# A transformer chain with experts on one core: runs of small passes placed more closely, the last layer's inverse roots on another engine, and one maximum read from PSUM

## The chip, the core and the metric

The kernel runs on one core of a Trainium2 chip. It has five engines that work side by side, each in the order of its own instruction stream: TensorE (PE: matmuls and transposes, results in PSUM), VectorE (DVE), ScalarE (ACT: activation functions, copies), GpSimd (POOL[...]) and SyncE (SP: DMA issue). The metric is the device time of one execution in microseconds (us). The time before is the median of three runs, 1779.1 us (1774.51 to 1781.71).

## The reference, cut to what matters

The input is `x`, 64 sequences of 64 tokens with 128 features, and a context `ctx` of the same shape. Four layers follow each other:

```python
# layer 0: self attention over [ctx, x] with 16 heads of 64 and relative positions, norm, relu feed-forward, norm
# layer 1: masked self attention, norm, masked cross attention with ctx, norm, relu feed-forward, norm (heads of 8)
# layer 2: gate between a token and its sequence's pooled context, softmax over the tokens, norm
# layer 3:
x = x + mha(ln(x), ln(x))                     # self, 16 heads of 8
x = x + mha(ln(x), ln(ctx))                   # cross, both sides normed
h = ln(x)
vals, idx = top_k(h @ rw.T + rb, 2)           # router: 2 of 8 experts
gates = softmax(vals)
x = x + sum over the 2 of gates * (gelu(h @ fc1[e].T + b1[e]) @ fc2[e].T + b2[e])

def ln(x): return (x - mean(x)) / sqrt(var(x) + 1e-5) * g + b
```

All arithmetic is float32.

## The kernel before

**Tiling.** The 4096 tokens are eight groups (`g` = 0 to 7) of 512: a tile `x0` to `x7` of 128 partitions by four blocks of 128 features. Layer 0 runs first with all engines held to program order. Everything after it is made of Python generators, driven by one function.

**The driver.** `drive` (L149) keeps two lists of tasks: "attention" (`self1`, `cross1`, `self3`, `cross3`, each for every group, all groups of one phase before the next phase) and "light" (`forward1`, `layer2`). A task is started every four or two turns of the loop, once the same group has finished its earlier phase. In each turn every running generator is advanced to its next `yield`, and the generator `experts` (called `fill`) is advanced once, or two and three times by turns after the last exponentials have been issued. So a `yield` sets how finely a task's instructions are mixed with those of others. The instructions so recorded then pass a planner that orders each engine's stream by the estimated readiness and the order of recording; the queues on the chip are in order.

**A norm.** `normalise` (L263) takes mean and variance of four blocks on VectorE, adds epsilon there, raises to the power -0.5 on GpSimd (`rs`, 128x4), multiplies the mean by it on VectorE (`nmr`) and scales on ScalarE (`z` or `zx`). It is used for all norms. In the last layer `ln_turned` (L1230) calls it for the self attention's input, and for the query and context of the cross attention; `cross3` (L1251) calls it once more for the router's input `zx`. That makes 32 calls of 80.

**Attention with small heads.** `small_heads` forms keys `km` and queries `qs` on ScalarE, scores in four PSUM banks (`sc`), and for each bank the maximum of each row (`mx`) and the difference. Without a mask (last layer), the first three banks are read by VectorE straight from PSUM; the fourth is copied by ScalarE to SBUF (`s`), VectorE takes the maximum from that copy and GpSimd subtracts. The weights are turned on TensorE (`pt`), ScalarE takes the exponential (`pT`), and `av` multiplies them with the values.

**Router and experts.** `router` (L1279) takes the logits (`pl`), the two largest, the gates, each token's row in a table of experts (`pr` counts by a triangular matmul), and scatters the rows to `hrows` in DRAM: eight indirect DMAs per group, issued by GpSimd. `experts` (L649) waits until groups 0 to 4 have been routed, makes a `table` of 47 blocks of 128 rows, waits until the last group's exponentials have been issued, and then handles one block in each step: a load from `hrows` (SyncE), a transpose (`xt`), `f<-fcw,vp` (first matmul), transposes (`ht`), Gelu on ScalarE, the second matmul, and a scatter to `yrows` by GpSimd out of one of six result buffers. A second table of 31 blocks follows when groups 5 to 7 have been routed. Finished rows are read back, summed with `x` and written out.

Nearly all instructions carry line L74 in the profile, since one helper issues them; the groups are told apart by the names of their tiles.

Of the kernel before, what the change touches and what calls it, by code (L numbers as in the profile page):

```python
# [12 lines left out]
AF = mybir.ActivationFunctionType  # L13
# [3 lines left out]
P = 128  # L17
# [77 lines left out]
def kernel(ctx: ExitStack, tc: tile.TileContext, a: dict, out: bass.AP):  # L95
# [13 lines left out]
    def ctile(shape, name, dtype=F32):  # L109
        return const.tile(shape, dtype, tag=name, name=name)  # L110
# [34 lines left out]
    def mid(ap, n):  # L145

        return ap.unsqueeze(1).to_broadcast([ap.shape[0], n, ap.shape[1]])

    def drive(phases, lags, ends, fill):  # L149

        todo = {kind: [] for kind in lags}
        for n, (start, kind) in enumerate(phases):
            for g in range(NG):
                todo[kind].append((n, g, start))

        todo["light"].sort(key=lambda task: task[1])
        passed = {(-1, g) for g in range(NG)} - {(-1, g) for g, gen in ends}
        count = 0
        running, wait = [(-1, g, gen) for g, gen in ends], {kind: 0 for kind in lags}
        while running or any(todo.values()):
            for kind, tasks in todo.items():
                if wait[kind] <= 0:
                    for task in tasks:
                        n, g, start = task
                        if (n - 1, g) in passed:  # L170
                            tasks.remove(task)
                            running.append((n, g, start(g)))
                            wait[kind] = lags[kind] - (kind == "attention" and not todo["light"])
                            break
                wait[kind] -= 1
            for task in list(running):
                n, g, gen = task
                if next(gen, "end") == "end":
                    running.remove(task)
                    passed.add((n, g))  # L180
            count += 1
            for _ in range(2 + count % 2 if done["exponentials"] else 1):
                next(fill, "end")
        for _ in fill:
            pass

# [15 lines left out]
    make_identity(nc, ident[:, :])  # L202
    nhalf = ctile([P, NBLK], "nhalf")
    nc.gpsimd.memset(nhalf, -0.5)
    xs = [ctile([P, T], f"x{g}") for g in range(NG)]
    bd_small = ctile([P, 6, 8], "bd_small")
    bd = ctile([P, 6, P], "bd")
# [52 lines left out]
        nc.scalar.copy(t, pt)  # L260
        return t

    def normalise(dst, src, npm=None, width=D):  # L263

        st = wtile([P, NBLK, 6], "st6", 4)
        mv = wtile([P, NBLK, 2], "mv", 4)
        rs = wtile([P, NBLK], "rs", 4)
        for k in range(NBLK):
            nc.vector.bn_stats(st[:, k, :], src[:, k * P : (k + 1) * P])
        for k in range(NBLK):  # L270
            nc.vector.bn_aggr(mv[:, k, :], st[:, k, :])
        nc.vector.tensor_scalar(
            rs, mv[:, :, 1:2].rearrange("p a b -> p (a b)"), EPS, None, ALU.add
        )
        nc.gpsimd.tensor_tensor(rs, rs, nhalf, ALU.pow)
        if npm is not None:
            nc.gpsimd.tensor_tensor(rs, rs, npm, ALU.mult)
        yield
        if npm is None:
            nm = wtile([P, NBLK], "nmr", 4)  # L280
            nc.vector.scalar_tensor_tensor(
                nm, mv[:, :, 0:1].rearrange("p a b -> p (a b)"), -1.0, rs, op0=ALU.mult, op1=ALU.mult
            )
        for k in range(NBLK):
            ks = slice(k * P, (k + 1) * P)
            if npm is None:
                nc.scalar.activation(
                    dst[:, k * width : k * width + D], src[:, ks], AF.Identity,
                    scale=rs[:, k : k + 1], bias=nm[:, k : k + 1],
                )  # L290
            else:
                nc.vector.tensor_scalar(
                    dst[:, ks], src[:, ks], mv[:, k, 0:1], rs[:, k : k + 1], ALU.subtract, ALU.mult
                )
# [354 lines left out]
    def experts():  # L649
# [160 lines left out]

        while done["routed"] < PARTS[0]:
            yield
        yield from table(0)
        while not done["exponentials"]:
            yield

# [5 lines left out]
        for t in range(-6, total + 3):  # L822
# [1 line left out]
            while h < NH and done["routed"] < sum(PARTS[: h + 1]):  # L824
                yield
            if h < NH and h not in tables:
                yield from table(h)
            if t + 6 < total:
                load(t + 6)
            if 0 <= t < total:  # L830
# [25 lines left out]
    def other_layers(ends):  # L856
# [65 lines left out]
        def small_heads(qT, kvT, wq, wk, wv, wo, scale, bias=None, maskb=None, then=None):  # L922
# [28 lines left out]
            def scores(hb):  # L951
# [13 lines left out]
                for g in (3, 0, 1, 2):  # L965
# [10 lines left out]
                    elif g == 3:  # L976
                        nc.scalar.copy(s, s3)
                    if maskb is not None or g == 3:
                        nc.vector.tensor_reduce(mx, s, axis=AX.X, op=ALU.max)
                        nc.gpsimd.tensor_tensor(s, s, last(mx[:, :], S), ALU.subtract)  # L980
                    else:
                        nc.vector.tensor_reduce(mx, s3, axis=AX.X, op=ALU.max)
# [247 lines left out]
        def ln_turned(src, g, b, z=None):  # L1230

            z = wtile([P, T], "z", 3) if z is None else z
            yield from normalise(z, src)
            yield
            pt = transpose4(z)
            t = wtile([P, T], "T", 4)
# [14 lines left out]
        def cross3(g):  # L1251
# [16 lines left out]
            yield  # L1268

            zx = wtile([P, NBLK, ROWW], "zx", 4)  # L1270
            yield from normalise(zx.rearrange("p k c -> p (k c)"), x, width=ROWW)
            yield
            pt = transpose4(zx.rearrange("p k c -> p (k c)"), ROWW)
            hT = wtile([P, T], "T", 4)
            nc.scalar.activation(hT, pt, AF.Identity, scale=col("moe_g"), bias=col("moe_b"))
            yield
            yield from router(g, hT, x, zx)

        def router(g, hT, x, zx):  # L1279

# [220 lines left out]
```

## Time and profile before

| what | value |
|---|---|
| median of three runs | 1779.1 us |
| the profiled execution's own time | 1766.36 us |
| its span in the profile | 1764.6 us |
| granted TensorE clock, mean | 0.943 |
| busy: TensorE, its weight loads | 1617.1 us (92%), 1166.4 us (66%) |
| busy: VectorE, ScalarE, GpSimd | 1214.6 (69%), 991.9 (56%), 913.1 us (52%) |
| `pow` of the norms on GpSimd | 80, 1020 ns each |
| table loads on ScalarE | 2, 1283 ns each |

The profile lists for each engine the busy time and for each group of like instructions: line, engine, operation, output and inputs by the program's names, shape, count, then the busy time and mean duration, and after the second bar the idle time of that engine just ahead of these instructions with what ended it. A busy TensorE is not TensorE at its peak: the ends of matmuls are modelled. PEclk is the clock granted to TensorE; the records show 1.0 or 0.5 at any time. A table load (ACT_TABLE_LOAD) brings a set of functions into ScalarE; it is put into the stream by the compiler where the next function is not in the set that is loaded.

### The profile page before, as it was taken

What the parts mean: (1) busy time and instruction counts of PE and PEld (TensorE: products, weight loads), DVE (VectorE), ACT (ScalarE), POOL (GpSimd) and SP (SyncE); (2) the same over time, 40 slices, a digit from 0 to 9 for tenths busy, and PEclk for the clock granted to TensorE, in tenths of its full rate; (3) what the DMA queues carried; (4) which work ended last, traced back from release to release, by engine and by line L of the source; (5) the groups of instructions that cost most, each with busy time, mean ns of one, the idle gap of its engine ahead of it and who ended that gap; (6) DMA issues with size and microseconds to landing.
All of it is one profiled execution on the core that took longest, in us unless ns stands there. A gap on an engine that the chain in (4) does not pass through costs nothing.

```text
span 1764.6 us, 46242 instructions
## 1 busy us (share of the span) xinstructions
PE 1617.1 (92%) x18026; PEld 1166.4 (66%) x18026; DVE 1214.6 (69%) x3289; ACT 991.9 (56%) x2712; POOL 913.1 (52%) x875
## 2 busy tenths in 40 slices
PE   7799999999999999699998999899888988679995
PEld 4466666666666666477776777667666767557774
DVE  4567686867676767578887786777566874556663
ACT  4365555556464646255665555567677853236663
POOL 2446373737374647467776666444222243554454
PEclk9899999999999999899999998899889987579998
DMA  6756555555545455410010000000000000112143
GB/s 160 159 142 158 127 142 132 136 138 131 139 128 141 132 147 153 138 49 8 11 32 25 23 20 8 13 2 2 8 14 14 2 20 20 55 51 56 54 122 89
DMA packets 215160, 136.78 MB, mean 78 GB/s; under 512 B 38896, under 2 KB 198786, under 8 KB 214816
## 3 DMA queue, kind: packets, MB, share of 16 engines
q1 hardware_dynamic: 186880, 90.54, 21.3%
q10 hardware_dynamic: 23520, 34.75, 6.0%
q0 software_dynamic: 4544, 8.54, 1.4%
q8 instruction: 144, 2.36, 0.6%
q14 instruction: 72, 0.59, 0.1%
HBM read 66.51 MB, written 68.19 MB: 76 GB/s over the span
## 4 chain that ended last, share of the span: by engine, by line
PE 64%; DVE 16%; ACT 7%; POOL 5%; issue 3%; DMA 3%; another core or an unknown queue 0%; SPq 0%; POOLq 0%; ACTq 0%; DVEq 0%
PE av L74 8%; PE psv L74 8%; PE proj L74 7%; PE psk L74 6%; PE pt L74 6%; PE f L74 6%; PE tok L74 5%; PE pbd L74 4%; DVE mx L74 3%; PE psc L74 3%; DVE s L74 3%; PE acc L74 3%; PE sc L74 3%; ACT z L74 3%; PE tr L74 2%
## 5 line engine op out<-in xcount | busy, mean ns | idle before, releaser
L74 ACT ACTIVATE s<-s,nm 128x128 f32<-128x128 f32 x512 | 198.0, 388 | 248.9 <-DVE nm L74 218.7
L74 POOL TENSOR_TENSOR s<-s,sm 128x512 f32<-128x512 f32 x128 | 130.4, 1040 | 256.0 <-DVE sm L74 256.0
L74 PE MATMUL pt<-ident,s 128*128 128x128 f32 x1536 | 213.5, 282 | 24.5 <-ACT kT L74 10.4
L74 POOL TENSOR_TENSOR s<-s,mx 128x512 f32<-128x512 f32 x160 | 164.0, 1045 | 107.1 <-DVE mx L74 106.9
L74 PEld LDWEIGHTS pt<-ident,s 128*128 128x128 f32 x1536 | 176.4, 145 | 45.1 <-issue 15.2
L74 ACT ACTIVATE pT<-pt 128x512 f32<-128x512 f32 x256 | 141.7, 605 | 81.6 <-PE pt L74 76.9
L74 POOL TENSOR_TENSOR rs<-rs,nhalf 128x4 f32<-128x4 f32 x80 | 81.6, 1020 | 191.9 <-DVE rs L74 157.8
L74 POOL TENSOR_TENSOR skew<-skew,mb 128x512 f32<-128x512 f32 x128 | 159.9, 1271 | 37.0 <-DMA skew<-scr 36.5
L74 PEld LDWEIGHTS av<-vb,pT 128*64 128x64 f32 x4096 | 133.7, 144 | 21.2 <-issue 16.5
L74 PE MATMUL av<-vb,pT 128*64 128x18 f32 x4096 | 142.0, 216 | 4.7 <-issue 2.6
L74 DVE TENSOR_REDUCE mx<-s 128x8 f32<-128x512 f32 x160 | 102.9, 675 | 43.8 <-ACT s L74 43.8
L74 POOL DMA_INDIRECT yrows<-km,tob x78 | 76.2, 977 | 100.9 <-DVE m L74 75.3
L74 PE MATMUL psv<-wv,kv 128*128 128x256 f32 x512 | 127.4, 392 | 0.0
L74 PE MATMUL psk<-kv,wk 128*128 128x512 f32 x256 | 127.4, 620 | 0.0
L74 PE MATMUL sc<-km,qs 32*64 32x256 f32 x2048 | 104.7, 420 | 17.2 <-ACT qs L74 12.6
L74 DVE COPY pT<-pt 128x512 f32<-128x512 f32 x128 | 82.2, 683 | 37.5 <-PE pt L74 37.5
L74 PEld LDWEIGHTS psv<-wv,kv 128*128 128x128 f32 x512 | 92.2, 189 | 15.1 <-issue 1.0
L74 PEld LDWEIGHTS av<-pT,v 128*64 128x64 f32 x2048 | 66.6, 138 | 52.8 <-issue 31.1
L74 PEld LDWEIGHTS pbd<-rT,qp 64*128 64x128 f32 x1024 | 63.0, 189 | 58.0 <-DVE qp L74 56.3
L74 DVE TENSOR_TENSOR s<-sc,mb 128x512 f32<-128x512 f32 x128 | 81.9, 680 | 23.1 <-PE sc L74 23.1
L74 DVE TENSOR_TENSOR s<-psc,skew 128x512 f32<-128x512 f32 x128 | 87.5, 683 | 14.7 <-issue 7.3
L74 ACT ACTIVATE z<-z,nmr,rs 128x128 f32<-128x128 f32 x160 | 66.1, 488 | 55.7 <-DVE nmr L74 42.0
(237 smaller groups left out, 3749.0 us busy)
## 6 DMA issues: line engine op xcount, KB each, us to landing
scr<-stage SPq DMA_DIRECT2D x64, 516.0 KB
skew<-scr SPq DMA_DIRECT2D x128, 256.0 KB
hrows<-pad ACTq DMA_DIRECT2D x66, 330.0 KB
ctx<-in_ctxT SPq DMA_DIRECT2D x24, 256.0 KB
km<-hrows SPq DMA_DIRECT2D x78, 66.0 KB
fcw<-in_fc ACTq DMA_DIRECT2D x16, 256.0 KB
kv<-in_xT SPq DMA_DIRECT2D x8, 256.0 KB
kv<-in_ctxT SPq DMA_DIRECT2D x8, 256.0 KB
```

Of the source, the lines that this page charges most:

```text
L74: ins = it(*args, **kw)
```

## The change

There are three parts.

1. The driver knows a new word, `CHAIN`. A task that yields it is in a run of small passes: it is not advanced with the others but behind every second other piece of a turn, at the end of the turn, and behind every step of `experts`. The norm and transposes ahead of the router, the router itself and both tables are such runs.
2. `normalise` has a second way to the inverse root, `root="ln"`: Ln of variance plus epsilon and Exp with a scale of -0.5, both on ScalarE. The last layer's 32 norms use it.
3. The fourth bank's maximum, where there is no mask, is taken from PSUM and not from the copy.

```diff
+    CHAIN = "chain"
+
+    def chain(gen):
+        for _ in gen:
+            yield CHAIN
...
-        count = 0
+        count, chains, filling = 0, set(), [None]
         running, wait = [(-1, g, gen) for g, gen in ends], {kind: 0 for kind in lags}
+
+        def advance(task):
+            n, g, gen = task
+            said = next(gen, "end")
+            chains.discard(task)
+            if said == "end":
+                running.remove(task)
+                passed.add((n, g))
+            elif said == CHAIN:
+                chains.add(task)
+
+        def advance_chains():
+            for task in [task for task in running if task in chains]:
+                advance(task)
+            if filling[0] == CHAIN:
+                filling[0] = next(fill, "end")
+
...
+            beats = 0
             for task in list(running):
-                n, g, gen = task
-                if next(gen, "end") == "end":
-                    running.remove(task)
-                    passed.add((n, g))
+                if task not in chains:
+                    advance(task)
+                    beats += 1
+                    if beats % 2 == 0:
+                        advance_chains()
+            advance_chains()
             count += 1
             for _ in range(2 + count % 2 if done["exponentials"] else 1):
-                next(fill, "end")
+                if filling[0] != CHAIN:
+                    filling[0] = next(fill, "end")
+                    advance_chains()
...
+    eps = ctile([P, 1], "eps")
+    nc.gpsimd.memset(eps, EPS)
...
-    def normalise(dst, src, npm=None, width=D):
+    def normalise(dst, src, npm=None, width=D, root="pow"):
...
-        nc.vector.tensor_scalar(
-            rs, mv[:, :, 1:2].rearrange("p a b -> p (a b)"), EPS, None, ALU.add
-        )
-        nc.gpsimd.tensor_tensor(rs, rs, nhalf, ALU.pow)
+        var = mv[:, :, 1:2].rearrange("p a b -> p (a b)")
+        if root == "pow":
+            nc.vector.tensor_scalar(rs, var, EPS, None, ALU.add)
+            nc.gpsimd.tensor_tensor(rs, rs, nhalf, ALU.pow)
+        else:
+            nc.scalar.activation(rs, var, AF.Ln, bias=eps)
+            nc.scalar.activation(rs, rs, AF.Exp, scale=-0.5)
...
-        yield from table(0)
+        yield from chain(table(0))
...
-                yield from table(h)
+                yield from chain(table(h))
...
-                        nc.vector.tensor_reduce(mx, s, axis=AX.X, op=ALU.max)
+                        nc.vector.tensor_reduce(mx, s if maskb is not None else s3, axis=AX.X, op=ALU.max)
...
-            yield from normalise(z, src)
+            yield from normalise(z, src, root="ln")
...
-            yield from normalise(zx.rearrange("p k c -> p (k c)"), x, width=ROWW)
-            yield
+            yield CHAIN
+            yield from chain(normalise(zx.rearrange("p k c -> p (k c)"), x, width=ROWW, root="ln"))
+            yield CHAIN
...
-            yield
-            yield from router(g, hT, x, zx)
+            yield CHAIN
+            yield from chain(router(g, hT, x, zx))
```

## The prediction

> **What bounds the kernel now.** I read the page's 40 slices first, then the busy time of every engine by stage, then the waits of the densest stage, and last the timeline of the two places where the change acts.
>
> ```profile
> PE   7799999999999999699998999899888988679995
> ACT  4365555556464646255665555567677853236663
> PEclk9899999999999999899999998899889987579998
> ```
>
> TensorE (PE) is busy nearly everywhere up to the sixteenth slice, so the first layer is TensorE's; the change does not touch it. From about slice 27 ScalarE (ACT) rises to 6, 7 and 8 tenths, then falls to 2 and 3, where TensorE's clock falls to 7 and 5 tenths as well. Cut into stages (start:end in us, then busy us and count for PE, its weight loads, DVE, ACT, POOL, then the clock):
>
> ```profile
> core 0: us, PE busy (x) PEld busy (x) DVE busy (x) ACT busy (x) POOL busy (x), PEclk, DMA share, GB/s
> 1075.00:1275.00 200.00, 181.37 (x2187) 132.06 (x2193) 136.80 (x385) 127.94 (x254) 83.56 (x72) 0.91 0.02 7
> 1275.00:1425.00 150.00, 137.06 (x2105) 106.33 (x2090) 107.22 (x383) 117.62 (x233) 44.51 (x42) 0.92 0.03 9
> 1425.00:1498.00 73.00, 64.39 (x760) 51.67 (x756) 42.45 (x181) 29.42 (x57) 30.25 (x31) 0.76 0.07 24
> 1498.00:1537.00 39.00, 24.32 (x100) 18.65 (x98) 21.34 (x155) 6.25 (x15) 25.63 (x26) 0.50 0.16 50
> 1537.00:1600.00 63.00, 50.03 (x265) 35.92 (x266) 36.92 (x175) 25.53 (x82) 28.12 (x29) 0.80 0.19 53
> 1600.00:1700.00 100.00, 99.71 (x648) 76.22 (x647) 69.00 (x260) 64.96 (x214) 42.86 (x44) 1.00 0.27 74
> ```
>
> These are: the last layer's self attentions (with the end of the gates before them), its cross attentions (the dense stage), the draining of the last two, the hole between the last attention product (1498.1) and the first expert matmul (1537.2), the experts' slow start, and the experts at full pace. In the dense stage TensorE is busy 91% and ScalarE 78%: ScalarE has only 32.4 us of idle time there. In the hole nothing is busy: 39 us at half clock while routers and the slot table pass through short VectorE operations.
>
> The norms that change are 32: eight of the self attentions, sixteen of the cross attentions (context and query), eight ahead of the routers. Their `pow` on GpSimd starts, in the trace's order, at 1071 to 1246 us (8, self), 1276 to 1423 us (20: sixteen cross, four router) and 1448, 1478, 1499 and 1512 us (router).
>
> **The change, part by part.** The sum is against the profiled execution, 1764.6 us of span in a run of 1766.4 us; the runs shown have a median of 1779.1 us, 12.7 us above it, so I add the difference to the median.
>
> *Roots on ScalarE.* Removed: 32 additions on VectorE and 32 `pow` on GpSimd. Added on ScalarE: 32 Ln and 32 Exp on 128x4. And in the changed kernel as built, ScalarE's stream holds 70 table loads where the kernel before has 2: every Ln is preceded by a load of table set 5, the Exp after it by a load of set 0, and among the experts' Gelus (set 10) stand another few. The prices:
>
> ```profile
> L74 POOL TENSOR_TENSOR rs<-rs,nhalf 128x4 f32<-128x4 f32 x80 | 81.6, 1020 | 191.9 <-DVE rs L74 157.8
> L74 ACT ACT_TABLE_LOAD x2 | 2.6, 1283 | 5.9 <-DMA h<-in_wr 5.9
> L74 ACT ACTIVATE e<-e 128x4 f32<-128x4 f32 x8 | 1.7, 214 | 14.2 <-DVE e L74 6.9 <-DVE ci L74 4.1 <-DVE cum L74 3.1
> ```
>
> A norm thus takes 2 x 1.283 + 2 x 0.214 = 2.99 us of ScalarE instead of 1.02 us of GpSimd. GpSimd was idle most of that time (44.5 busy of 150 us in the dense stage), so its relief buys nothing there; 68 loads and 64 activations put 87.2 + 13.7 = 101 us on ScalarE.
>
> Here a rule weighs both ways. The Trainium skill, "ScalarE: Activation LUTs", section "Table sets: the hidden batching unit", says that Ln followed by Exp needs one load, since one named set holds both; then the 64 loads would shrink to a handful and this part would cost about 64 x 0.214 = 14 us of ScalarE, hidden. The built stream contradicts it: the Exp takes set 0 each time. I follow the stream. The section "What ACT_TABLE_LOAD costs" of the same page counts 2.66 us for a switch, 1.28 of load and 1.38 of drain. The trace has one load in running work:
>
> ```profile
> 1540.27 0.46 ACT L74 ACTIVATE vp<-xt,cols 128x128 f32<-128x128 f32 x1 [2.78 <-PE xt L74]
> 1540.74 1.28 ACT L74 ACT_TABLE_LOAD   x1
> 1542.19 1.14 ACT L74 ACTIVATE s<-ht,mb 128x128 f32<-128x128 f32 x4 [0.16 <-PE ht L74]
> ```
>
> It starts as the activation ahead of it ends, and the one behind starts 0.17 us after it, waiting for TensorE. No drain is to be seen, so I take 1.28; with 2.66 a norm would cost 5.75 us, the 68 loads 181 us, and this part alone some 150 us. A load can also run before the Ln has its data, as this one did; idle time of ScalarE can therefore swallow loads.
>
> By stage. Dense: 20 norms x 2.99 = 59.8 us on top of 117.6 makes 177.4 us of work in what was 150 us, so at least +27.4 us even if ScalarE never idled; at most +59.8. Of its 32.4 us of idle time 18.6 us is spent ahead of the norms' scaling of z, waiting for VectorE, and that wait stays; the other 13.8 can take loads. I take 59.8 - 13.8 = +46. Behind a delayed Ln on ScalarE stand the exponentials pT, and TensorE waits for those; the key projections km and qs too, and the score matmuls wait for those. Self stage: 8 norms, 23.9 us, with ScalarE idle 36% of the time; bounds 0 and +24, taken +8. Drain: two router norms stand between the last exponentials; bounds 0 and +6, taken +4. Together +58, from +27 to +90.
>
> *Fourth tile's maximum from PSUM.* 32 reductions read PSUM instead of ScalarE's copy. The durations do not differ:
>
> ```profile
> L74 DVE TENSOR_REDUCE mx<-s 128x8 f32<-128x512 f32 x160 | 102.9, 675 | 43.8 <-ACT s L74 43.8
> L74 DVE TENSOR_REDUCE mx<-sc 128x8 f32<-128x512 f32 x96 | 62.6, 679 | 0.0
> ```
>
> It removes up to 43.8 us of VectorE's idle time, but the copy stays, GpSimd's subtraction still waits for it, and VectorE (107 of 150 us) is not the bound. I take -3, between -10 and 0.
>
> *Runs of small passes move on more often.* No instruction is added; on TensorE, ScalarE, VectorE and GpSimd the order changes from the first self norm on, and SyncE's is the same. Before, in TensorE's order, the matmuls of the last two routers and of the table stand between the last attention product and the first expert; after, the table's matmul stands ahead of the last product, and the first expert's transposes directly behind it. Before:
>
> ```profile
> 1518.99 1.88 PE L74 MATMUL pl<-rw,T 128*128 128x8 f32 x8 [0.87 <-issue]
> 1525.88 1.91 PE L74 MATMUL pb<-hotb,fc1bT 8*128 8x47 f32 x8 [5.01 <-DVE pT L74]
> ...
> 1535.32 0.69 PE L74 MATMUL xt<-ident,km 128*128 128x128 f32 x2
> 1537.19 1.22 PE L74 MATMUL f<-fcw,vp 128*128 x1 [1.18 <-ACT vp L74]
> ```
>
> At full pace an expert block takes 2.30 us. The last first-matmul of a block starts at 1741.5, so 77 blocks back a start without loss would have been 1741.5 - 177.1 = 1564.4, 66 us behind the last attention product: 39 us of hole and 27 us lost afterwards. 14 us of that is one gap from 1553.5 to 1567.7, where VectorE waits 10.5 us for a result buffer whose scatter stands behind 12 router scatters, one each 1.26 us, on GpSimd's queue. After the change I expect the first block about 5 us behind the last product (a norm's tail and one `vp` of 0.46 stand on ScalarE ahead of it). Still to be done beside the first 14 blocks: two routers, whose 16 scatters occupy GpSimd for 20 us, their VectorE chains, and 8 extra table loads, 10.3 us; the Gelus and with them the second matmuls queue behind those. I put the loss at 18 us instead of 27: start at 23 us, gain 43. The table's 23 short VectorE operations, one each 0.1 us or so, now run during the draining: +3. Together -40; at the best (no loss but 10 us) -52, at the worst (the gap on GpSimd's queue stays and the loads are on the path: 27 + 10 + 5 = 42 lost, and the drain delayed by the moved chains by 9) -15.
>
> *Sum:* +58 - 3 - 40 = +15: span about 1780, median of the runs 1779.1 + 15 = 1794 us.
>
> **The rivals.** (1) *Loads vanish in idle time*, so that the change is faster: ScalarE reaches full occupation, the dense stage costs its +27 and the other stages nothing, and the tail gives 47: 27 - 3 - 47 = -23, 1756 us. It decides once the norms cost less than 43 us in all. For it: the load above that ran ahead of its Gelu's wait. Against: ScalarE is strictly in order, and 18.6 us of its idle time is waiting for norms. (2) *Nothing is swallowed*: +90 - 3 - 40 = +47, 1826 us. For it: pairs of cross norms start 1.5 us apart (1275.8 and 1277.2), so four loads come in one bundle of 6 us and stall TensorE through the exponentials, perhaps into half clock. (3) *The tail only moves its gap*: the experts start early and then wait for GpSimd's scatters or the Gelus' loads; 58 - 3 - 15 = +40, 1819 us. (4) *They cancel*: norms +43, tail -40, 1779 us.
>
> **How the numbers follow.** This kernel's three runs span 7 us, so 0.5% (9 us) is about what can be told from no change. Chances: the forecast 0.42 (its own range 1783 to 1811), rival 1 0.24, rival 2 0.10, rival 3 0.11, rival 4 0.13. Faster takes rival 1 less its upper edge, 0.23; same is rival 4 with the edges of the forecast and of rival 1, 0.16; slower is the rest, 0.61. The range leaves out the lower part of rival 1 and the upper part of rival 2: 1753 to 1830.
>
> **What would show it.** Right: about 70 ACT_TABLE_LOAD of 1.28 us; ScalarE over 88% busy between the first cross norm and the last; that stage some 45 us longer; `pow` x48; the first f matmul within 10 us of the last av; the maximum of the fourth tile no longer waiting for ScalarE. Wrong: an activation after a load that starts over 1 us late without waiting for data (a drain), a dense stage that has not grown, or a gap above 10 us in TensorE's f matmuls.

## The result, and the profile after

The changed kernel takes 1847.1 us (median of five runs) against 1777.1 us of the kernel before: ratio 1.0404, 95% interval 1.0367 to 1.0442. The prediction had 1794 us, with a range of 1753 to 1830 us: the direction was right, and the time lies outside the range.

The comparison was made on one chip. On two other chips the same two kernels gave 1.0285 (1.0267 to 1.0302) and 1.0327 (1.0292 to 1.0362), with the kernel before at 1741.5 and 1738.2 us; how the chips differ is one of the findings below, and why they do stays open. I call the chip of the first comparison the first chip, since its number is not on record, and the others by their numbers.

The three rows of the page that answer to those shown of before, of the changed kernel on the first chip:

```profile
PE   7799999999999997899989998998778787768996
ACT  4456555655565553466555666687898764355663
PEclk9999999999999999999999998898887766588998
```

From slice 29 to slice 35 TensorE is at 7 and 8 tenths while its clock falls from 8 to 5; the short, deep dip of before (7, 5 and 7 in slices 34 to 36) has become a long decline. By stage (start:end in us, then busy us and count of each engine, then TensorE's clock), for the self attentions, the cross attentions (dense stage), the draining, the hole, and the experts' first 90 us:

```profile
core 0: us, PE busy (x) PEld busy (x) DVE busy (x) ACT busy (x) POOL busy (x), PEclk, DMA share, GB/s
1075.00:1294.00 219.00, 198.14 (x2294) 146.10 (x2294) 131.04 (x393) 156.50 (x295) 76.26 (x65) 0.87 0.02 5
1294.00:1488.00 194.00, 154.37 (x1895) 119.17 (x1896) 102.97 (x377) 161.98 (x289) 38.07 (x36) 0.77 0.04 12
1488.00:1598.00 110.00, 85.26 (x900) 70.38 (x899) 55.15 (x243) 50.35 (x88) 30.57 (x31) 0.66 0.06 19
1598.00:1610.00 12.00, 7.37 (x31) 5.71 (x31) 4.00 (x25) 2.28 (x4) 6.70 (x7) 0.50 0.26 74
1610.00:1700.00 90.00, 67.11 (x382) 50.18 (x383) 51.42 (x251) 49.06 (x131) 35.03 (x36) 0.81 0.15 43
```

The dense stage is where ScalarE is now the busiest engine (162 of 194 us, TensorE 154 us). The hole has shrunk to 12 us. But the draining ahead of it has grown to 110 us at a clock of 0.66, and the first 90 us of the experts have TensorE busy for 67 us only.

To compare runs, I cut each trace at the same five records: the first scaling of a self norm, the first scaling of a cross norm, the last one, the end of the last attention product, and the first expert matmul. In us:

```
run            chip    self  dense  draining  hole   tail    span
before         first  203.1  146.4    74.8    38.8  227.4  1764.6
after          first  219.0  194.0   109.8    11.9  239.3  1849.1
difference            +15.9  +47.6   +35.0   -26.9  +11.9   +84.5
before_again   8      203.3  146.5    67.4    34.3  214.3  1742.9
after_again    8      213.5  185.4    93.2     4.7  217.4  1794.1
difference            +10.2  +38.9   +25.8   -29.6   +3.1   +51.2
```

(On the first chip the profiled run of before was 11 us below its median and that of after 4 us above; so the spans differ by 84.5 us there and the medians by 70.) The dense stage ends with the end of the last scaling. The tail is all that follows the first expert matmul.

The groups that changed, as the changed kernel's trace has them (busy us and mean ns of one; then idle time before them and what ended it):

```profile
L74 ACT ACT_TABLE_LOAD x70 | 89.8, 1283 | 7.8 <-DMA h<-in_wr 6.5
L74 ACT ACTIVATE rs<-mv,eps 128x4 f32<-128x4 f32 x32 | 9.4, 297 | 6.0 <-DVE mv L74 5.7
L74 ACT ACTIVATE rs<-rs 128x4 f32<-128x4 f32 x32 | 6.5, 204 | 0.3
L74 POOL TENSOR_TENSOR rs<-rs,nhalf 128x4 f32<-128x4 f32 x48 | 49.5, 1031 | 97.5 <-DVE rs L74 93.0
L74 DVE TENSOR_REDUCE mx<-sc 128x8 f32<-128x512 f32 x128 | 81.9, 681 | 50.0 <-ACT s L74 50.0
```

The 70 loads, the 32 Ln (`rs<-mv,eps`), the 32 Exp and the 48 `pow` are as counted. The last row is a surprise: the maxima that now read PSUM still wait for ScalarE's copy, 50.0 us in all against 43.8 us before. Of the 32 edited reductions 25 waited, and each of them starts 0.03 us after the end of the copy; all 32 carry a wait on ScalarE's semaphore in the built program. Why they carry it is not shown. One norm on ScalarE's timeline (start, duration):

```profile
1474.74 1.28 ACT L74 ACT_TABLE_LOAD   x1
1476.03 0.30 ACT L74 ACTIVATE rs<-mv,eps 128x4 f32<-128x4 f32 x1
1476.35 1.28 ACT L74 ACT_TABLE_LOAD   x1
1477.64 0.20 ACT L74 ACTIVATE rs<-rs 128x4 f32<-128x4 f32 x1
```

Each activation starts 0.01 us after its load ends. No drain is to be seen.

TensorE at the hole:

```profile
1594.17 3.61 PE L74 MATMUL av<-vb,pT 128*64 128x18 f32 x64 [1.21 <-DVE before L74]
...
1600.82 1.01 PE L74 MATMUL pgt<-ident,gates 128*8 128x128 f32 x4 [1.57 <-issue]
1603.51 1.88 PE L74 MATMUL pl<-rw,T 128*128 128x8 f32 x8 [1.67 <-ACT T L74]
...
1607.72 2.07 PE L74 MATMUL tok<-fc2b,T 8*128 8x128 f32 x8 [1.39 <-DVE T L74]
1609.71 2.08 PE L74 MATMUL f<-fcw,vp 128*128 x2
```

Only one router and the end of another stand there now. And the last attention product itself waited 1.21 us for VectorE's `before` (a router's counts).

The first matmuls of expert blocks on either side of the two longest gaps between them:

```profile
1623.60 1.02 PE L74 MATMUL f<-fcw,vp 128*128 x2
...
1638.29 2.07 PE L74 MATMUL f<-fcw,vp 128*128 x2
...
1655.37 1.02 PE L74 MATMUL f<-fcw,vp 128*128 x2
...
1672.20 2.08 PE L74 MATMUL f<-fcw,vp 128*128 x2
```

These are two gaps of 14.7 and 16.8 us, where before has one of 14.1 us; the prediction had named a gap above 10 us as a sign that it is wrong. The last two routers' scatters run in both (1621 to 1633 and 1655 to 1665 us). On chip 8 the longest such gap of after is 7.6 us.

### The profile page after: what moved, and what is told of

Same layout as the page of the kernel before. It is cut to its first block, busy times and chain, and to the rows that moved or that the text cites. A ratio compares the mean times of both kernels' runs of the same rounds, so it can differ in the third digit from the quotient of the medians.

```text
span 1849.1 us, 46245 instructions
## 1 busy us (share of the span) xinstructions
PE 1657.8 (90%) x18026; PEld 1201.9 (65%) x18026; DVE 1200.1 (65%) x3257; ACT 1096.2 (59%) x2844; POOL 880.3 (48%) x844
## 5 line engine op out<-in xcount | busy, mean ns | idle before, releaser
L74 PE MATMUL pt<-ident,s 128*128 128x128 f32 x1536 | 222.3, 290 | 30.4 <-DVE mx L74 16.8
L74 PEld LDWEIGHTS pt<-ident,s 128*128 128x128 f32 x1536 | 185.4, 150 | 50.1 <-issue 18.0
L74 PEld LDWEIGHTS av<-vb,pT 128*64 128x64 f32 x4096 | 142.9, 152 | 27.3 <-issue 17.4
L74 PE MATMUL av<-vb,pT 128*64 128x18 f32 x4096 | 150.9, 222 | 5.9 <-DVE before L74 3.0
L74 DVE TENSOR_REDUCE mx<-sc 128x8 f32<-128x512 f32 x128 | 81.9, 681 | 50.0 <-ACT s L74 50.0
L74 DVE COPY pT<-pt 128x512 f32<-128x512 f32 x128 | 82.1, 682 | 37.5 <-PE pt L74 37.5
L74 DVE TENSOR_TENSOR s<-psc,skew 128x512 f32<-128x512 f32 x128 | 87.3, 682 | 14.7 <-issue 6.8
L74 POOL TENSOR_TENSOR rs<-rs,nhalf 128x4 f32<-128x4 f32 x48 | 49.5, 1031 | 97.5 <-DVE rs L74 93.0
L74 ACT ACTIVATION_READ_ACCUMULATOR s<-s,nm 128x1 f32 x512 | 95.5, 187 | 0.0
```

What stands on the lines that cost most here:

```text
L74: ins = it(*args, **kw)
```

## The experiments

Two theories stood against each other for the +35 us of the draining and the missing tail gain. Theory A: the table loads hold up ScalarE there too. Theory B: the moved routers and table stand on the in-order queues between the pieces of the last attentions. (The 85 and 122 us of the draining in the expectations are from cuts that start 10 to 13 us earlier than those of the tables here.) The stage table of all runs; each row is one profiled execution, and those of max_only (7 us), set6_only (6 us), after_third (5 us) and chain_router (13 us) lie that much above their medians:

```
run              chip   self  dense  draining  hole   tail    span
chain_pow        4     206.6  171.9    94.2     6.9  217.3  1775.4
ln_only          4     208.9  186.9    65.0    34.4  212.6  1785.6
ln_noload        4     196.9  156.5    82.6     6.9  217.2  1733.4
max_only         4     210.2  148.3    68.1    34.2  215.3  1755.8
set6             8     206.7  156.5    82.4     4.7  216.1  1745.3
set6_only        8     206.1  145.9    64.8    34.4  213.7  1744.9
chain_router     7     210.2  177.1   102.2    16.0  231.7  1817.0
chain_table      7     203.0  149.1    82.4    43.3  222.1  1778.4
late6            7     203.4  149.1    82.5    37.5  232.3  1781.0
set6_nomax       7     199.8  173.3   109.1    15.3  238.1  1814.5
after_third     13     215.9  187.0    93.8     6.9  217.1  1801.2
set6_third      13     209.8  156.5    82.4     4.7  216.0  1745.0
chain_pow_third 13     206.6  171.9    94.2     6.9  217.6  1775.9
set6_twice      13     206.4  156.7    84.5     7.3  236.4  1768.2
mix              6     208.7  153.9   102.5    15.7  238.7  1796.1
late6_mix        6     208.7  134.2    81.4    32.5  237.2  1767.9
```

### Each part alone

**chain_pow**: the changed kernel with `pow` for all norms.

```diff
-            yield from normalise(z, src, root="ln")
+            yield from normalise(z, src, root="pow")
-            yield from chain(normalise(..., x, width=ROWW, root="ln"))
+            yield from chain(normalise(..., x, width=ROWW, root="pow"))
```

> The changed kernel with the 32 norms' roots put back on GpSimd (pow): the moved small passes and the fourth tile's maximum alone. Theory A (the table loads hold up ScalarE through the draining of the last attentions too, which grew by 37 us): the draining is as long as before, some 85 us, the tail keeps its gain of 15 us or more, 1735 to 1765 us. Theory B (the moved routers and tables stand between the pieces of the last attentions on the in-order queues): the draining stays near 122 us, and the kernel is slower than before, 1790 to 1805 us.

Measured: 1.0221 (1.0192 to 1.0250), 38 us more than the kernel before on the same chip; theory B had +13 to +28, theory A a gain, so the loss is above both. Again on chip 13:

> The changed kernel with pow for all norms: moved passes and fourth tile. 1.022 on a chip of the second kind, where half of it was the routers' pow behind another router's scatters on GpSimd's queue; on a chip of the first kind the engines are held by the same scatters anyway, so 1.022 to 1.035.

Measured: 1.0208 (1.0185 to 1.0231). Theory B holds in direction: without any of the norms' loads the dense stage is 25 us longer than in before_again, the draining 27 us, and the hole 27 us shorter. Part of that has a cause of its own. Waits of VectorE, ScalarE and TensorE in the dense stage (us in total, times, longest), of chain_pow:

```profile
DVE nmr L74 <- POOL rs L74: 23.9, 12, 7.0
ACT zx L74 <- DVE nmr L74: 16.7, 3, 7.9
PE tok L74 <- DVE T L74: 15.6, 2, 7.9
```

In max_only, where the routers keep their pace, the first of these is 12.8 us in 13 waits, the longest 1.2 us. GpSimd's timeline in chain_pow shows why:

```profile
1397.62 0.96 POOL L74 DMA_INDIRECT hrows<-zx,to  x1 [0.30 <-issue]
...
1402.35 0.98 POOL L74 DMA_INDIRECT hrows<-zx,to  x1 [0.17 <-issue]
1403.63 0.96 POOL L74 DMA_INDIRECT hrows<-zx,to  x1 [0.30 <-issue]
1404.89 0.96 POOL L74 DMA_INDIRECT hrows<-zx,to  x1 [0.30 <-issue]
1405.87 1.06 POOL L74 TENSOR_TENSOR rs<-rs,nhalf 128x4 f32<-128x4 f32 x1
```

A router's norm now falls into the time in which the previous router's scatters are being issued, and its `pow` stands behind them. `nmr` on VectorE waits for it, and behind `nmr` stand in order the copies `T` that TensorE's `tok` waits for.

**ln_only**: the kernel before with Ln and Exp for the 32 norms, nothing else.

```diff
-        nc.gpsimd.tensor_tensor(rs, rs, nhalf, ALU.pow)
+            nc.scalar.activation(rs, var, AF.Ln, bias=eps)
+            nc.scalar.activation(rs, rs, AF.Exp, scale=-0.5)
```

> The kernel before with Ln and Exp on ScalarE for the same 32 norms, nothing else. Theory A: self stage +13, dense stage +48, draining +37: 1865 to 1885 us. Theory B: self and dense stage only, draining +5: 1835 to 1850 us. Were the 64 loads swallowed by idle time: 1775 to 1790 us.

Measured: 1.0280 (1.0251 to 1.0308), 1789.1 us. Against before_again the self stage is +5.6, the dense stage +40.4, the draining -2.4 us. The draining does not grow with the norms alone: theory A is out for them. (All expectations of these four were reckoned in us from 1777 us, but chip 4 runs the kernel before in 1740.8 us. Taken from there it is +48 us, where theory B had +58 to +73 and swallowed loads +13 at most: between the two.)

**ln_noload**: the changed kernel with the Ln replaced by an Exp, so that 10 loads remain.

```diff
-            nc.scalar.activation(rs, var, AF.Ln, bias=eps)
+            nc.scalar.activation(rs, var, AF.Exp, bias=eps)
```

> The changed kernel with each Ln replaced by an Exp on the same operands (the logarithm is left out, so the norms scale by other numbers): the same activations in the same places, but 10 table loads instead of 70. If the loads are the cost, the dense stage falls back to some 140 us and self stage and dense stage give up some 60 us: 1785 to 1795 us with theory B, 1740 to 1770 us with theory A. If it is the two dependent activations waiting in ScalarE's queue, it stays above 1830 us.

Measured: 0.9965 (0.9946 to 0.9985), 1735.2 us, 6 us less than the kernel before on this chip. The activations in ScalarE's queue cost nothing that can be told; the loads are the cost. In us it is nearer to theory A, which had a gain of 7 to 37 us, than to B's loss of 8 to 18; but A had no growth of the draining, and it is 82.6 us here, against 67.4 us. Both had left out what the rows above show, that `pow` on GpSimd is a bad neighbour of the moved scatters. With `pow`, chain_pow is 44 us longer than this kernel, but only 27 us of that lie in the dense stage and the draining, where the scatters are; 15 us lie ahead of them, in the self stage and before it, and are not explained by this. Since the logarithm is left out, the results are not the reference's; set6 below has both functions. On chip 13 chain_pow_third is 28 us above set6_third, 27 us of it in the same two stages.

**max_only**: the kernel before with the fourth tile's edit.

```diff
-                        nc.vector.tensor_reduce(mx, s, axis=AX.X, op=ALU.max)
+                        nc.vector.tensor_reduce(mx, s if maskb is not None else s3, axis=AX.X, op=ALU.max)
```

> The kernel before with the fourth tile's maximum read from PSUM, nothing else. In the changed kernel's trace these reductions still wait for ScalarE's copy (50.0 us in all), so nothing is gained: within 3 us of the kernel before. The prediction had -3 (from -10 to 0).

Measured: 1.0048 (1.0031 to 1.0065), some 8 us slower and so a miss. Its waits for the copy are 45.2 us against 43.2 us of before_again: nothing was removed. In the profiles the self stage is the one that grew most. First max_only, then before_again:

```profile
1079.70:1289.90 210.20, 191.73 (x2260) 140.60 (x2258) 138.98 (x403) 130.59 (x257) 85.59 (x73) 0.88 0.02 7
```

```profile
1077.10:1280.40 203.30, 184.19 (x2262) 134.15 (x2258) 139.61 (x403) 129.71 (x258) 85.59 (x73) 0.91 0.02 7
```

Nearly the same matmuls took 7.5 us longer at a granted clock of 0.88 instead of 0.91, and the stage is 6.9 us longer. But the two profiles come from two chips, and that of max_only is the slowest of its seven runs, so the place of the loss is less sure than its size. The edit also changes the order of other instructions, on TensorE (`psv` and `pt`) and more so on VectorE. That the order lowers the clock is argued, not shown by a run of its own; the kernels set6_nomax and mix, which leave the edit out, ran on chips that differ in more than this.

### The loads taken away, with the right numbers

**before_again** and **after_again** are the two kernels unchanged, for profiles on the same chip.

> The kernel before, unchanged, for a profile from the same chip as the three beside it. The four single edits ran on another chip than the first comparison, where the kernel before took 1740.8 us instead of 1777 us. Expected: a ratio of 1.000; its trace shows whether the hole behind the last attention product (39 us) and the slow start of the experts look the same there.

Measured: 0.9993 (0.9982 to 1.0004).

> The changed kernel, unchanged, on the same chip as the others of this call. Ratio 1.040 as in the first comparison; the single edits (moved passes with pow 1.022, Ln and Exp alone 1.028, fourth tile alone 1.005) would add up to about 1.050 if they were independent.

Measured: 1.0285 (1.0267 to 1.0302), less than the 1.050 of the parts.

**set6**: the changed kernel, which loads by hand, ahead of a Ln or of a router's Exp, the table set that holds both functions, where another set was in use.

```diff
+    def table_set(name):
+        if held[0] != name:
+            if name == "natural_log_exp_and_others":
+                load = nc.scalar.preload_act_table_set(name)
...
+            table_set("natural_log_exp_and_others")
             nc.scalar.activation(rs, var, AF.Ln, bias=eps)
```

> The changed kernel with the table set that holds both Ln and Exp loaded by hand ahead of a norm where another set is active: 23 table loads instead of 70, none between the cross attentions, and the same activations with the same results. If the loads are what the norms cost (and the odd numbers of the kernel without the logarithm had nothing to do with its time), this falls to the time of that kernel plus 13 loads x 1.28 = 17 us at most: ratio 0.997 to 1.007. If the activations' place in ScalarE's queue is the cost, it stays above 1.03.

Measured: 1.0023 (1.0015 to 1.0032), 1744.4 us. The trace has `ACT_TABLE_LOAD x23`. Of the 23 loads, 13 stand in the self stage and 9 among the experts. Against after_again, 47 loads fewer are worth 48.1 us, 1.02 us each of the 1.283 us that one takes. On chip 13 the same pair:

> The changed kernel, unchanged, beside the next three on one chip. 1.040 where the engines stand still during scatters (first comparison), 1.0285 where they do not.

> The changed kernel with 23 instead of 70 table loads, as before. The 47 loads are worth 2.6% of the time on the chip measured; if that is the same everywhere, 1.040 becomes 1.015 to 1.025 on a chip of the first kind, and the rest is the moved passes with their scatters. On a chip of the second kind 1.002.

Measured: 1.0327 (1.0292 to 1.0362) and 1.0051 (1.0034 to 1.0067); 50.7 us, or 1.08 us per load. Both ratios are some 0.3 to 0.4% above what was expected of this chip.

**set6_only**: ln_only with the set loaded by hand, 15 loads instead of 64.

> The kernel before with Ln and Exp on ScalarE and the set that holds both loaded by hand: 15 table loads instead of 64. If the loads are the cost: ratio 0.995 to 1.008, against 1.028 with the 64 loads. If it comes out below 0.99, the relief of GpSimd's queue is worth something by itself, without the moved passes.

Measured: 0.9999 (0.9988 to 1.0010). Norms on ScalarE without the loads cost nothing and bring nothing; GpSimd's relief by itself is worth nothing.

What is left in set6 is the moved passes, the fourth tile's edit and 23 loads, of which 15 cost nothing in set6_only. Dense stage and draining of before_again, then of set6:

```profile
1280.40:1426.80 146.40, 133.48 (x1987) 103.16 (x1984) 104.34 (x361) 116.09 (x228) 42.27 (x40) 0.92 0.03 9
1426.80:1494.20 67.40, 57.87 (x812) 49.06 (x808) 44.12 (x185) 30.40 (x60) 31.51 (x32) 0.84 0.08 26
```

```profile
1285.70:1442.20 156.50, 140.43 (x1957) 110.85 (x1956) 102.88 (x377) 117.74 (x256) 38.01 (x36) 0.86 0.05 15
1442.20:1524.60 82.40, 69.88 (x899) 59.94 (x898) 55.34 (x243) 39.58 (x80) 31.48 (x32) 0.80 0.08 26
```

The hole fell by 29.6 us; the dense stage rose by 10.1 us, of which 7 us is TensorE taking longer for fewer matmuls at a clock of 0.86 instead of 0.92, and the draining by 15.0 us. It now holds 243 VectorE operations instead of 185 and 899 matmuls instead of 812: the routers' and the table's. From the first cross norm to the first expert it is 248.2 us before and 243.6 us after. The passes were moved from a place where nothing else ran to a place where they are in the way.

### Which passes, and an order in which they might gain

These four ran on chip 7, where the kernel before takes 1772.4 us, near the first chip's time. **chain_router** (both tables at their old pace) and **chain_table** (only the tables at the new pace, with the maximum from the copy); both have `pow` for all norms, and a cut of each edit is shown:

```diff
-        yield from chain(table(0))
+        yield from table(0)
```

> The changed kernel with pow for all norms and with only the last norms and routers moving on more often; the slot table's passes are as before. If the routers are what lengthens the dense stage and the draining and what empties the hole, this stays near the 1.022 of both together, with the hole a few us longer: 1.020 to 1.028. If the table's 23 operations ahead of the last attention were the cost, it falls to 1.005 or less.

Measured: 1.0180 (1.0148 to 1.0211), just below what was expected; the hole is 16.0 us.

```diff
-            yield CHAIN
-            yield from chain(router(g, hT, x, zx))
+            yield
+            yield from router(g, hT, x, zx)
```

> The kernel before with only the slot table's passes moving on more often (pow, maximum from the copy). The table waits for the fifth router, which is as late as before, so the hole behind the last attention product stays above 25 us: ratio 0.995 to 1.003. If the table alone closed the hole: 0.985.

Measured: 1.0035 (1.0011 to 1.0058), and the hole stays at 43.3 us. The routers make nearly all of it, in gain and loss (chain_router has the fourth tile's edit with them).

**late6**: tables and last two routers only, `pow`, maximum from the copy. It has one thing more: each of the last two groups waits with its router's norm until all groups before it have been routed.

```diff
+            while g >= 6 and done["routed"] < g:
+                yield
...
+            said = CHAIN if g >= 6 else None
-            yield from chain(router(g, hT, x, zx))
+            yield from chain(router(g, hT, x, zx), said)
```

> The kernel before with the table's passes and those of the last two routers (seventh and eighth) moving on more often, the first six as before, pow for all. The hole shrinks, from 34 us to some 15 to 20, since its passes stand between the first expert blocks, and no router burst lies in the dense stage or ahead of the last attention pieces: ratio 0.988 to 0.995. If moving routers only shifts the loss into the experts' start: 0.998 to 1.005.

Measured: 1.0048 (1.0032 to 1.0064), a miss for the first branch and within the second. The dense stage stays at 149 us, but the hole is 37.5 us: it did not shrink. The added wait of the last two routers may be why; no run without it tells.

**set6_nomax**: set6 without the fourth tile's edit.

> The changed kernel with the set that holds Ln and Exp loaded by hand, and without the fourth tile's edit. If that edit costs what it cost alone (+0.48%, through TensorE's clock in the self stage): 1.002 - 0.005 = 0.997. If its cost was an accident of that one order of instructions: 1.002.

Measured: 1.0215 (1.0186 to 1.0245), a miss by far. Dense stage, draining and tail are 173.3, 109.1 and 238.1 us instead of set6's 156.5, 82.4 and 216.1: the moved passes, without the fourth tile's edit, cost more on this chip than with it on chips 8 and 13. The next part has what the traces show of the reason.

**mix** (set6_nomax with `pow` for the self norms, 11 loads) and **late6_mix** (the same, only the last two routers and the tables moved, with late6's added wait), on chip 6, where the kernel before takes 1764.8 us:

> The changed kernel with pow for the self attentions' norms (which alternate with a Tanh of another table set), Ln and Exp from the one set that holds both for cross attentions and routers, and the maximum from the copy: 11 table loads. Against the kernel with 23 loads (1.002 to 1.005) it saves 3 us of loads and whatever the fourth tile's edit costs: 0.995 to 1.001 on a chip that doesn't stand still during scatters, 1.018 on one that does.

Measured: 1.0175 (1.0120 to 1.0230), the number expected for a chip on which the engines stand still.

> As the run beside it, but only the last two routers and the table move on more often. If the routers moved into the dense stage and the draining are what eats the gain, both stages stay near 146 and 67 us, the hole falls to about 20 us, and the ratio is 0.988 to 0.994. If the hole doesn't shrink because the eighth attention is waited for anyway: 0.998 to 1.003.

Measured: 1.0010 (0.9994 to 1.0025), as for a hole that does not shrink: it is 32.5 us. The dense stage falls to 134.2 us; the draining with 81.4 us and the tail with 237.2 us take that back (before on the first chip: 146.4, 74.8 and 227.4). No version with the right results was faster than the kernel before.

### Chips on which engines stand still while scatters are issued

In after on the first chip, during a router's eight scatters:

```profile
1562.09 1.55 PE L74 MATMUL av<-vb,pT 128*64 128x18 f32 x47
...
1568.85 0.96 POOL L74 DMA_INDIRECT hrows<-zx,to  x1 [0.30 <-issue]
1570.12 0.95 POOL L74 DMA_INDIRECT hrows<-zx,to  x1 [0.30 <-issue]
1571.38 0.96 POOL L74 DMA_INDIRECT hrows<-zx,to  x1 [0.30 <-issue]
1572.53 0.36 DVE L74 RECIPROCAL rec<-av 128x32 f32<-128x32 f32 x1 [7.79 <-remote]
...
1573.40 0.47 PE L74 MATMUL tr<-ident,o 128*128 128x128 f32 x1 [7.27 <-DVE o L74]
```

The product `av` ended at 1563.6; the reciprocal that needs it started at 1572.53, 0.2 us after the last scatter had been issued, and TensorE and ScalarE stood still as well. The profile finds no work that released it ("remote"). The same place in after_again on chip 8:

```profile
1545.93 3.04 PE L74 MATMUL av<-vb,pT 128*64 128x18 f32 x64 [2.36 <-DVE before L74]
...
1548.14 0.95 POOL L74 DMA_INDIRECT hrows<-zx,to  x1 [0.30 <-issue]
1549.01 0.36 DVE L74 RECIPROCAL rec<-av 128x32 f32<-128x32 f32 x1 [0.34 <-PE av L74]
1549.40 0.96 POOL L74 DMA_INDIRECT hrows<-zx,to  x1 [0.30 <-issue]
```

It starts 0.04 us after the product, with scatters going on all the while. Such delays can be counted: a signal of TensorE, VectorE or ScalarE after 1200 us whose record comes over 1.5 us behind the end of the instruction that sends it, and ahead of the end of the next one that sends the same signal. On the first chip there are 21 in before (70 us in sum, overlapping) and 37 in after (143 us), on chips 6 and 7 16 to 24 in every run, and on chips 4, 8 and 13 none to two in every trace. In nearly all of them a scatter is being issued (19 of 21, 35 of 37), and up to 1370 us, ahead of the first scatter, no trace has one. On the chips that show delays the records of some 5% of these signals are missing from 1200 us on (139 of 2461 in before), so the counts are rough; on the others hardly one is, and up to 1370 us none or two on any chip. So the recording itself is a rival for the cause, and no run tells the two apart.

The delays fit what the kernel before shows: its 1765 to 1777 us on the first kind of chip and 1738 to 1742 us on the second differ in draining, hole and tail (74.8, 38.8, 227.4 against 67.4, 34.3, 214.3), where the scatters are, and not in the self and dense stages.

So before had its late scatters in a hole where little else runs, and the change moves them beside the attentions and the experts. With Ln and Exp and most loads taken away, the moved passes cost 0.2 to 0.5% on chips of the second kind (set6, with the fourth tile's edit) and 1.75 to 2.15% on those of the first (mix, set6_nomax, without it); none of these kernels ran on both kinds. With `pow` there is no such difference: chain_pow costs 2.1 to 2.2% on the second kind, and chain_router, the same but for the tables' pace, 1.8% on the first.

**set6_twice** issues each scatter twice, the second time to a table that nobody reads.

```diff
+                    sp = nc.gpsimd.indirect_dma_start(
+                        out=spare[PLACE[g][0]][:, :], out_offset=bass.IndirectOffsetOnAxis(ap=to[:, k : k + 1], axis=0),
+                        in_=zx[:, k, :], in_offset=None,
+                    )
```

> The kernel with 23 table loads, and each router's eight scatters issued twice, the second time to a table that nobody reads (the output does not change): 64 more scatters of 1.26 us on GpSimd. If scatters hold the other engines up: some 30 to 60 us more than the kernel with 23 loads, with stretches of about 12 us in which TensorE, VectorE and ScalarE all stand still. If GpSimd's idle time takes them and only its own queue is longer: less than 15 us more.

Measured on chip 13, one of the second kind: 1.0171 (1.0149 to 1.0194), 21.9 us above set6_third. Neither expectation holds: dense stage and draining did not grow (+0.2 and +2.1 us), and 20.4 us went into the tail, where the experts' own result scatters stand behind them on GpSimd, and VectorE waits for these to land (the second fence; the helper's line is L77 in this kernel):

```profile
1439.90:1524.40 84.50, 71.51 (x899) 61.32 (x897) 54.44 (x235) 39.62 (x81) 54.97 (x57) 0.77 0.14 43
...
1531.80:1600.00 68.20, 51.35 (x292) 37.66 (x292) 41.19 (x215) 40.10 (x103) 51.08 (x54) 0.85 0.23 68
```

```profile
1596.96 0.21 DVE L77 TENSOR_SCALAR tob<-m,km 128x1 uint32<-128x1 f32 x1 [12.70 <-DMA yrows<-km,tob]
```

GpSimd is busy 51 of the experts' first 68 us, against 37 us in set6_third. On such a chip the extra scatters cost 2.3 us beside the attentions, and beside the experts they cost their queue's time; TensorE, VectorE and ScalarE stand still together for 10 us ahead of this wait's end, with no late signal there. That it is the scatters that hold the engines on the other kind rests on the coincidence in the traces; the doubling did not fall on such a chip, and what makes the chips differ is open.

## Why the prediction was wrong, point by point

*The failed step* is the moved passes: "start at 23 us, gain 43 ... Together -40". With 47 of the 70 loads taken away, the moved passes and the fourth tile's edit together cost +2.9 us on chip 8 (set6) instead of gaining 43; on the first kind of chip the moved passes cost 1.75 to 2.15% without that edit (mix, set6_nomax, 11 and 23 loads; no single edit ran on the first chip itself, and chips 6 and 7 stand for it). I had costed what left the hole and not what it would meet: for the table "+3", for the routers that move into the dense stage and the draining nothing, and 9 us only at the worst. The draining was set at +4 us, for two norms' loads. It grew by 35.0 us on the first chip and by 25.8 us on chip 8, where set6 shows 15.0 us without most loads and the other 10.8 us come with them. The hole itself shrank as said, to 11.9 us on the first chip and 4.7 on chip 8 (I had 5). "In the hole nothing is busy" was a misreading of my own row: TensorE is busy 24.3 of its 39 us, VectorE 21.3 and GpSimd 25.6. The routers and the table are that work, and it still had to be done in another place.

*The slow start of the experts*, which I let fall from 27 to 18 us, did not fall. By the same reckoning (77 blocks of 2.30 us back from the last one) it lost 39.5 us on the first chip and 17.5 us on chip 8, where the kernel before loses 14.2 us. So some half of the 27 us is not there on chip 8: the wait of 10.5 us that I read as one for a result buffer ends with 4.7 us (1562.4 to 1567.1 us) in which TensorE, VectorE and ScalarE all stand still, and the profile finds no work that released it; the gap of 14.1 us around it is 9.0 us on chip 8. The gain on the first chip was thus 66 - 11.9 - 39.5 = 15 us, and not 43, nor the 24 us of my worst case ("-15" is these less 9 us for the draining); of the draining I allowed 9 us and had 35.

*The norms* were right in mechanism and nearly in size; the direction of the whole came right through them. "+46" for the dense stage: ln_only gives +40.4 (chip 4 against before_again on chip 8, two chips of the second kind), so 19.4 us of 59.8 were swallowed and not 13.8. The measured +47.6 us of the first chip looks closer than it is, since moved passes are in it. Self: "+8", alone +5.6. No drain behind a load: right. ScalarE "over 88% busy": 83% (87% on chip 8). Their sum, "+58", is 48 us by ln_only and 48 to 51 us by the two pairs with and without 47 of the loads.

*The rule of the Trainium skill* ("ScalarE: Activation LUTs", "Table sets: the hidden batching unit") that Ln and Exp share a load was set aside for the stream as built, rightly: 70 loads ran. Loaded by hand, one set does serve both, and the price that I worked out for that case (14 us of ScalarE, hidden) fits set6_only: 0.9999.

*The fourth tile*, "-3", was +8 us alone; what it costs beside the other parts no run shows by itself. The wait that it was to remove stayed (50.0 us), so "the maximum of the fourth tile no longer waiting for ScalarE" was wrong.

*The rivals.* Rival 3 (the tail moves its gap, 1819) has the right mechanism, but its "-15" was too good: on the first chip hole, tail and draining together gave +20 us. Rival 2 (nothing swallowed) had +90 us for the norms, where 48 to 51 were measured, and took the same -40; that its 1826 us comes nearer to the time is luck. Rival 1 failed as to the loads: 80 to 84% of each load's time lay on the path. Rival 4 took the -40 as well.

## What to carry to other kernels

Price a moved chain twice: what its old place gains, and what each of its instructions meets on the in-order queues of its new place, its DMA issues included. When functions on ScalarE alternate, count the loads in the built stream, and see whether a set loaded by hand holds both: here it was worth 2.6 to 2.8%. Before a result is generalised, look whether another chip shows it: of the 70 us lost on the first chip, 51 and 60 us were lost on the two others.

## What was not expected of the hardware

On the first chip and on chips 6 and 7 signals of TensorE, VectorE and ScalarE came late by up to 14 us while GpSimd issued indirect scatters of 0.96 us each, and in after all three stood still together for 3 to 6 us at a time; on chips 4, 8 and 13 the signals came in time but for one or two. The kernel before is 1.3 to 2.2% slower on the former. Cause and link are open.

A table load of 1.283 us cost 1.02 to 1.08 us of the kernel's time where ScalarE was busy 83 to 87% of the dense stage, although TensorE and not ScalarE was the busiest engine before.
